# Layer 2's first tasks: half 1's sums to GpSimd, small products and weight sums later, values copied ahead of keys

## The chip, the core and the metric

The kernel runs on one core of a Trainium2 chip. The core has five engines, each with its own in-order instruction queue: TensorE (PE, matrix products; its weight loads are listed as PEld), VectorE (DVE), ScalarE (ACT), GpSimd (POOL) and SyncE (SP, which here only starts DMAs). They meet through semaphores. PE writes its results into PSUM, a small memory of eight banks; here each bank has a letter (S, U, T, V, X, Y, Z, W). DVE and ACT read PSUM; POOL does not. Everything else lies in SBUF or in device memory. The metric is the time of one execution in microseconds (us) of the device; lower is better.

## The reference, cut to what matters

Four transformer layers work on x, of 4 sequences of 256 tokens with 512 features, in fp32. In each, `x = x + attention(norm(x)) + ffn(norm(x))`. The change concerns layer 2 alone:

```python
# attention: 32 query heads, 8 key/value heads of 128 features, rotary, causal
qkv = einsum('bsh,oh->bso', xn, Wqkv)
xq, xk = rope(xq), rope(xk)
probs = softmax(where(causal, xq @ xk.T / sqrt(128), -1e30))
attn = (probs @ xv) @ Wo.T
# ffn: a dense product, and a mixture of 8 experts of rank 16
result = einsum('bsd,od->bso', xn, W_base) + b_base
ax = einsum('bsd,rd->bsr', xn, A_w)
probs = softmax(einsum('bsd,ed->bse', xn, router_w))
mixed = einsum('bseq,bse->bsq', einsum('bsr,erq->bseq', ax, cores), probs)
result = result + einsum('bsr,or->bso', mixed, B_w) * 2
```

## The kernel before, in words

The normalised input lies transposed in `xT`, features on partitions, 1024 tokens along the free axis. Its tokens are cut into half 0 (sequences 0 and 1) and half 1 (sequences 2 and 3); tiles 0 to 3 of 128 tokens are half 0, tiles 4 to 7 half 1.

All large products of layer 2 are done as 2 by 2 blocks with seven block products instead of eight (L1121, `SEVEN`). Each needs sums of blocks on both sides. For the input they are `s1` to `s4` (`summed`, L1134, four 128x512 additions, called for a half by `block_sums`, L1242); for a weight they are `t1` to `t4` (`Blocks.sums`, four additions on POOL). The seven products go to banks X, Y, Z, W, X, Z, W. `quarters` (L1369) says how four result quarters come out of them: ACT copies X into `u` and Z into `z`, DVE adds Y to `u`, then makes `c` = u + W (`c22`), POOL adds z to it: that is quarter (1,1). Later X is quarter (0,0), and Z and W, after DVE has added u, are (0,1) and (1,0). A function `place` empties each quarter: for queries the rotary (three DVE instructions and one addition on POOL); for keys and values (`key_tasks`, L1508) the rotary of the keys (`rotary_by_four`: three DVE instructions, L1463 once and L1461 twice, then an addition on POOL, L1487) and one ACT copy of the values (L1512). Keys and values of one quarter share a bank, and a tile `kv`, of which each takes a half.

The order of work on PE, DVE, ACT and POOL is written out by hand (`manual_schedule`, L1315): they execute in program order. SP is not in that list; a planner orders its DMAs. Program order comes from slots: `run` (L1929) takes a list of tasks, one a slot. In each slot it calls the task (a block product on PE), and then the functions that `after(k, f)` (L1350) has put down for that slot, k slots ahead, in the order in which they were put down. What the set-up puts down before the first slot therefore stands at the head of a slot's list. `spread(k, steps)` puts steps into successive slots.

Slots 0 to 6 are keys and values of key/value pair 0 for half 0 (`key_tasks(0, 0)`), slots 7 to 13 queries of half 0 (`query_tasks(0)`), slots 14 to 20 keys and values of half 1, 21 to 27 queries of half 1, 28 to 34 the base weight's output product of half 0. From slot 14 on attention runs beside this: `scores` of a head pair on PE in slot 14, 19, 24, 29, at once `masked` on DVE, a slot later `exponentials` on ACT, then `normalise`, then `turned_blocks` (DVE, and four DMAs on SP), then `values` on PE.

The first slots also carry what half 1 and the feed-forward part need: in slot 0 the moments of tiles 4 to 7 (DVE, and a square root on ACT); in slots 1 to 4 their normalisation (DVE), transposes (PE) and evacuation to `xT` (`turned`, L153; `evac`, L95, sends even tiles to DVE, odd ones to ACT); in slot 5 `route(1)` (the rank and router products for half 1: PE, and ACT's copy `flat`), in slot 6 `route_back(1)` and DVE's s1 and s2, in slot 7 s3 and s4, the router's softmax (`chosen`, L1960, with an exponential on ACT) and `core` (one product on PE, one ACT copy). Slots 8 to 11 hold eight DVE instructions `products` (L1970), slots 10 and 12 their transposes `turn_z` (L1979: four on PE, one ACT copy to `zT`), slots 6 to 9 POOL's sums of the base weight (`outs[0].sums()`). ACT's functions lie in sets; another set means a table load (ACT_TABLE_LOAD).

Of the kernel before, what the change touches and what calls it, by code (L numbers as in the profile page):

```python
# [21 lines left out]
F32 = mybir.dt.float32  # L22
# [4 lines left out]
AF = mybir.ActivationFunctionType  # L27
# [4 lines left out]
P = 128  # L32
B, T, C = 4, 256, 512
NT = B * T // P
# [22 lines left out]
def block_stack(ctx: ExitStack, tc: tile.TileContext, d: dict, out: bass.AP):  # L57
    nc = tc.nc

    const = ctx.enter_context(tc.tile_pool(name="const", bufs=1))  # L60
    small = ctx.enter_context(tc.tile_pool(name="small", bufs=4))
# [33 lines left out]
    def evac(i, dst, src):  # L95
        if i % 2:
            nc.scalar.copy(dst, src)
        else:
            nc.vector.tensor_copy(dst, src)
# [10 lines left out]
    xT = const.tile([P, NC, B * T], F32, name="xT")  # L110
# [18 lines left out]
    def moments(tiles):  # L129

        n = len(tiles)
        mv = small.tile([P, n, 2], F32, tag=f"mv{n}", name=f"mv_{tiles[0]}")
        for i, t in enumerate(tiles):
            st = small.tile([P, 6], F32, tag="st", name=f"st_{t}")
            nc.vector.bn_stats(st, x_sb[:, t, :])
            nc.vector.bn_aggr(mv[:, i, :], st)
        rstd = small.tile([P, n], F32, tag=f"rstd{n}", name=f"rstd_{tiles[0]}")
        nc.scalar.activation(rstd, mv[:, :, 1], AF.Sqrt, bias=eps, scale=1.0)
        nc.vector.reciprocal(rstd, rstd)
        return {t: (mv[:, i, 0:1], rstd[:, i : i + 1]) for i, t in enumerate(tiles)}  # L140

    def normed(t, moments, patterns):

        xn = lnp.tile([P, C], F32, tag="xn", name=f"xn_{t}")
        dst, src = xn, x_sb[:, t, :]
        if patterns:
            before, after, sizes = patterns
            dst = xn.rearrange(after, **sizes)
            src = src.rearrange(before, **sizes)
        nc.vector.tensor_scalar(dst, src, *moments[t], ALU.subtract, ALU.mult)  # L150
        return xn

    def turned(t, xn, tag="T"):  # L153

        tp = ps(tag, [P, NC, P], f"lnT_{t}")
        for c in range(NC):
            nc.tensor.transpose(tp[:, c, :], xn[:, c * P : (c + 1) * P], ident)
        evac(t, xT[:, :, t * P : (t + 1) * P], tp)


    def layer0_attention(hook, aside, xp, wd):
# [1025 lines left out]
    class Layer2Weights:  # L1187
# [51 lines left out]
                )  # L1239
            nc.scalar.copy(self.routed[:, 4 * half : 4 * half + 4, :], tp)  # L1240

        def block_sums(self, half):  # L1242
            A = self.A[half]
            for i in range(2):
                cols = slice((2 * half + i) * T, (2 * half + i + 1) * T)
                for j in range(2):
                    A[f"a{i + 1}{j + 1}"] = xT[:, 2 * j : 2 * j + 2, cols]
            return summed(
                nc.vector, A, lambda k: self.xs.tile([P, 2, T], F32, name=f"x_{k}_{half}")
            )  # L1250

        def first_half(self):
# [39 lines left out]
    def layers_2_and_3(w, late):  # L1292
# [8 lines left out]
        with ExitStack() as stack:  # L1301
# [25 lines left out]
            def tile2(tag, bufs, name):  # L1327
                pool = rp if tag in ("kv", "u", "z", "c", "t2") else lp
                return pool.tile([P, 2, T], F32, tag=tag, name=name, bufs=bufs)
# [8 lines left out]
            A = w.A  # L1338

            def turn_tile(t, mom):  # L1340
                turned(t, normed(t, mom, None), "TVSY"[t % 4])

            row = tile2("kv", 13, "b2_row").rearrange("p a i -> p (a i)")
            nc.sync.dma_start(out=row, in_=bc(d["b2"], 0, P))
# [5 lines left out]
            def after(k, *fs):  # L1350

                due.setdefault(slot[0] + k, []).extend(fs)
# [118 lines left out]
            def rotary_by_four(dst, src):  # L1471


                t2 = tile2("t2", 2, "t2")[:, 0, :]

                def natural(x):
                    return x.rearrange("p (x i b) -> p x b i", x=2, b=4)

                rotated(
                    dst.rearrange("p (x b i) -> p x b i", x=2, b=4),  # L1480
                    natural(src),
                    natural(rope[:, 0, :]),
                    natural(rope[:, 1, :]),
                    t2.rearrange("p (x b i) -> p x b i", x=2, b=4),
                    0,
                )
                after(1, lambda: nc.gpsimd.tensor_tensor(dst, dst, t2, ALU.add))  # L1487
# [20 lines left out]
            def key_tasks(gp, half):  # L1508
                def place(c, src):
                    t = kv[gp, half, c] = tile2("kv", 13, f"kv2_{gp}_{half}_{c[0]}{c[1]}")  # L1510
                    rotary_by_four(t[:, 0, :], src[:, 0, :])
                    nc.scalar.copy(t[:, 1, :], src[:, 1, :])  # L1512

                return quarters(lambda: A[half], lambda: w.sets["kv", gp].b, keys_values, place)

# [36 lines left out]
            class Layer3:  # L1552
# [241 lines left out]
                def turned(self, t, j, tag):  # L1794
                    half, i, tt = t // 4, t % 4 // 2, t % 2
                    A = self.retrieval[half]
                    tp = ps(tag, [P, 4, P], f"retT_{t}_{j}")
                    for k in range(4):
                        nc.tensor.transpose(tp[:, k, :], self.rets[t][4 * j + k], ident)  # L1799
                    key = f"a{i + 1}{j + 1}"  # L1800
                    if key not in A:
                        A[key] = self.rt[half].tile(
                            [P, 4, T], F32, tag="rt", name=f"rt_{half}_{key}", bufs=7
                        )
                    nc.vector.tensor_copy(A[key][:, :, tt * P : (tt + 1) * P], tp)
# [110 lines left out]
            def spread(k, steps):  # L1916

                for i, f in enumerate(steps):
                    after(k + i, f)
# [37 lines left out]
            zT = [tile2("kv", 13, f"zT_{i}").rearrange("p a i -> p (a i)") for i in range(2)]  # L1957
            core_out = tile2("kv", 13, "core_out_sb").rearrange("p a i -> p (a i)")

            def chosen():  # L1960
                nc.vector.tensor_reduce(most, probs, AX.X, ALU.max)
                nc.vector.tensor_tensor(probs, probs, bc(most, 2, EXPERTS), ALU.subtract)
                nc.scalar.activation(probs, probs, AF.Exp)
                nc.vector.tensor_reduce(most, probs, AX.X, ALU.add)
                nc.vector.reciprocal(most, most)
                nc.vector.tensor_tensor(probs, probs, bc(most, 2, EXPERTS), ALU.mult)
# [43 lines left out]
            def biased(t):  # L2010
                nc.gpsimd.tensor_tensor(x_sb[:, t, :], x_sb[:, t, :], row, ALU.add)

            half1 = {}
            after(0, lambda: half1.update(mom=moments(range(4, NT))))
            for i, t in enumerate(range(4, NT)):
                after(1 + i, lambda t=t: turn_tile(t, half1["mom"]))
            after(5, lambda: w.route(1, "U"), lambda: half1.update(sums=w.block_sums(1)))
            for i in range(4):
                after(6 + i // 2, lambda i=i: half1["sums"][i]())
            after(6, lambda: w.route_back(1, "S"))  # L2020
            after(7, chosen, core)
            for g in range(2):
                for i in range(4):
                    after(8 + 2 * g + i // 2, lambda t=4 * g + i: products(t))
                after(10 + 2 * g, lambda g=g: turn_z(g))
            spread(6, outs[0].sums())
            run(key_tasks(0, 0) + query_tasks(0))

            def next_set():
# [353 lines left out]
```

## Time and profile before

| What | us |
|---|---|
| Runs of the kernel | 1346.69, 1344.92, 1344.08 (median 1344.92) |
| Profiled execution | 1343.17 |
| its span on the core | 1341.4 |
| layer 2's first product (slot 0) starts | 488.21 |
| first queries (slot 7) start | 504.33 |
| first scores (slot 14) start | 523.71 |
| base weight's first product (slot 28) starts | 554.71 |

The table's slots are found in the timeline by the names of what a product writes and reads: `m<-xT,wkv_b` is a product of keys and values, `m<-xT,wq_b` one of queries, `s<-kv,q` scores, `m<-wo_b,xT` the output product. A timeline's line gives start, duration, engine, source line, operation, tiles, shapes, and in brackets the engine's idle time ahead of it with what ended it. Instructions of an engine overlap a little, so a duration is often some 0.1 us longer than the distance to the next start.

### The profile page before, as it was taken

How to read it: one execution, taken by the hardware profiler on the slowest of the kernel's cores; microseconds unless marked ns; L12 is line 12 of the kernel's file. 1: busy time of each engine (PE TensorE's matmuls, PEld its weight loads, DVE VectorE, ACT ScalarE, POOL GpSimd, SP SyncE). 2: the span in 40 equal slices, each digit the busy share in tenths (PEclk: the TensorE clock that was granted, in tenths of full speed). 3: DMA queues.
4: the chain of work that ended last, by engine and by line, in shares of the span. 5: the costliest groups of instructions: out<-in, count | busy, mean ns of one | idle time of the engine just before them, and what ended most of it. 6: DMA issues, size and time to landing. Idle time of an engine off the chain costs nothing. (4 is left out here: it accounts for less than half of the span.)

```text
span 1341.4 us, 20444 instructions
## 1 busy us (share of the span) xinstructions
PE 1300.8 (97%) x7076; PEld 1022.7 (76%) x7076; DVE 928.9 (69%) x1962; ACT 561.2 (42%) x1475; POOL 656.7 (49%) x662
## 2 busy tenths in 40 slices
PE   9999999899998998999999999999999999899998
PEld 7666665688445677888888888888888888677887
DVE  6676777488836449837877967777678776768654
ACT  2444445387012212433444443444534444655530
POOL 4555566478646014654575745747356563021410
PEclk9999999999999999999999999999999999999999
DMA  6012112300610021222433424433334333413001
GB/s 222 6 48 48 37 48 76 87 1 21 177 46 9 0 95 52 75 71 63 131 98 95 126 61 118 115 95 102 87 91 119 94 78 82 145 24 118 1 1 63
DMA packets 93480, 101.47 MB, mean 76 GB/s; under 512 B 21748, under 2 KB 66535, under 8 KB 92994
## 3 DMA queue, kind: packets, MB, share of 16 engines
q1 hardware_dynamic: 92450, 99.12, 26.1%
q8 instruction: 56, 0.92, 0.3%
q10 hardware_dynamic: 816, 0.79, 0.2%
q14 instruction: 46, 0.38, 0.1%
q0 software_dynamic: 112, 0.26, 0.1%
HBM read 67.06 MB, written 7.91 MB: 56 GB/s over the span
## 5 line engine op out<-in xcount | busy, mean ns | idle before, releaser
L1859 ACT ACTIVATE p<-p,nm 128x256 f32<-128x256 f32 (+1 forms) x256 | 113.3, 444 | 158.8 <-DVE nm L1843 158.0
L1456 POOL TENSOR_TENSOR q<-q,t 128x512 f32<-128x512 f32 x64 | 81.9, 1280 | 130.3 <-DVE t L1461 128.5
L1874 ACT ACTIVATE p<-p,rs 128x256 f32<-128x256 f32 (+1 forms) x256 | 95.5, 444 | 39.9 <-DVE rs L1870 39.9
L1406 PE MATMUL m<-xT,wq_b 128*128 128x256 f32 x448 | 103.9, 380 | 2.1 <-ACT kv L1512 2.0
L1461 DVE TENSOR_TENSOR t<-m,rope_sb 64x512 f32<-64x512 f32 (+1 forms) x144 | 95.3, 662 | 1.9
L1406 PEld LDWEIGHTS m<-xT,wq_b 128*128 128x128 f32 x448 | 82.6, 191 | 12.6 <-ACT kv L1512 2.4
L1389 POOL TENSOR_TENSOR c<-c,z 128x512 f32<-128x512 f32 x28 | 36.4, 1301 | 112.9 <-DVE c L1386 57.9
L1882 DVE STREAM_TRANSPOSE blocks<-p 128x768 f32<-128x768 f32 x64 | 62.6, 977 | 40.1 <-ACT p L1874 39.1
L1442 PE MATMUL m<-wo_b,o 128*128 128x256 f32 x384 | 89.6, 380 | 0.0
L1910 ACT COPY o<-av 128x512 f32<-128x512 f32 x64 | 37.2, 582 | 115.6 <-PE av L1900 110.1
L1843 DVE CUSTOM_DVE_ANT_0 p<-s,cmask 128x256 f32<-128x256 f32 (+1 forms) x256 | 76.1, 353 | 12.8 <-PE s L1824 11.1
L1521 DVE TENSOR_TENSOR x_sb<-x_sb,m 128x512 f32<-128x512 f32 x82 | 54.8, 679 | 36.6 <-PE m L1442 25.3
L1442 PEld LDWEIGHTS m<-wo_b,o 128*128 128x128 f32 x384 | 72.0, 191 | 9.1
L786 PE MATMUL dn<-wd,hT 128*128 128x512 f32 x176 | 76.4, 594 | 0.7 <-ACT o L782 0.7
L1406 PE MATMUL m<-x_s,wq_t 128*128 128x256 f32 x320 | 74.1, 381 | 2.4 <-ACT kv L1512 2.0
L843 POOL TENSOR_TENSOR sa<-sa,sb 128x1024 f32<-128x1024 f32 x22 | 62.1, 2824 | 29.0 <-DVE sb L838 29.0
L476 POOL TENSOR_SCALAR_AFFINE_SELECT keys<-keys 128x256 f32<-128x256 f32 x128 | 58.1, 467 | 28.9 <-ACT keys L472 28.8
L472 ACT ACTIVATE keys<-st 128x384 f32<-128x384 f32 x128 | 54.0, 488 | 40.1 <-PE st L462 40.1
L1406 PEld LDWEIGHTS m<-x_s,wq_t 128*128 128x128 f32 x320 | 60.3, 191 | 11.9 <-ACT kv L1512 2.4
L1899 PE MATMUL av<-q,kv 128*128 128x512 f32 x128 | 65.5, 594 | 1.6 <-DMA q<-blocks 1.6
L1824 PE MATMUL s<-kv,q 128*128 128x256 f32 x256 | 65.8, 380 | 0.4 <-POOL q L1456 0.4
L786 PEld LDWEIGHTS dn<-wd,hT 128*128 128x128 f32 x176 | 33.3, 190 | 41.1 <-issue 39.4
(329 smaller groups left out, 3272.9 us busy)
## 6 DMA issues: line engine op xcount, KB each, us to landing
q<-blocks SPq DMA_DIRECT2D x256, 96.0 KB
wq_b<-in_wq SPq DMA_DIRECT2D x38, 256.0 KB
wo_b<-in_wo SPq DMA_DIRECT2D x32, 256.0 KB
raw<-in_wo SPq DMA_DIRECT2D x24, 256.0 KB
wkv_b<-in_wkv SPq DMA_DIRECT2D x16, 256.0 KB
wos_d<-wos_row SPq DMA_DIRECT2D x28, 128.0 KB
gate_q<-in_gate_q SPq DMA_DIRECT2D x11, 256.0 KB
up_q<-in_up_q SPq DMA_DIRECT2D x11, 256.0 KB
```

The costliest lines, as they stand in the source:

```text
L786: nc.tensor.matmul(po, lhsT=hT[:, k, t * P : (t + 1) * P], rhs=wd[:, k, :], start=k == 0, stop=k == NBLK - 1,)
L843: nc.gpsimd.tensor_tensor(self.a, self.a, self.b, ALU.add)
L1406: nc.tensor.matmul(out[:, i, :], lhsT=b[:, c, i * P : (i + 1) * P], rhs=a[:, c, :], start=start and i == 0 and c == 0, stop=i == 1 and c == 1,
L1442: nc.tensor.matmul(out[:, t, :], lhsT=a[:, c, t * P : (t + 1) * P], rhs=b[:, c, :], start=start and t == 0 and c == 0, stop=t == 1 and c = ...
L1456: after(1 + 2 * pause, lambda: nc.gpsimd.tensor_tensor(dst, dst, t2, ALU.add))
L1461: nc.vector.tensor_tensor(t2[at], src[of], sin[of], ALU.mult)
L1824: nc.tensor.matmul(s1[:, i, :], lhsT=q[:, i, P:T], rhs=kt[:, 0, :], start=True, stop=True)
L1843: nc.vector.tensor_tensor_reduce(out=x[f"p{part}"][:, e, :], in0=x[f"s{part}"][:, e, :], in1=cmask if part else cmask[:, P : 2 * P], scale ...
L1859: nc.scalar.activation(p, p, AF.Exp, bias=x["nm"][:, part, e : e + 1], scale=-1.0, accum_out=x["sums"][:, part, e : e + 1],)
L1874: nc.scalar.activation(p, p, AF.Copy, scale=x["rs"][:, part, e : e + 1])
L1882: nc.vector.transpose(blocks, x["p"].rearrange("p e x (b i) -> p b (e x) i", b=4))
L1899: nc.tensor.matmul(av, lhsT=v[:, 0:P], rhs=q[:, :, :, 0:64], start=True, stop=False)
```

## The change

Seven edits, all in what the first slots of layer 2 hold:

- the evacuations of tiles 4 to 7 all go to ACT (`turned` takes the engine as `by`);
- a tiny exponential on ACT follows the moments in slot 0 (`begun`);
- `s1` to `s4` of half 1 go from DVE to POOL, and from slots 6 and 7 to slots 8 to 11;
- the router's softmax is cut in two: maximum, difference and exponential (`raised`) stay in slot 7, the sum and the division (`chosen`) go to slot 9;
- the eight `products` go to slots 11 to 18, one a slot, and the two `turn_z` to slots 16 and 20;
- the base weight's sums go to slots 15 to 18;
- for key/value pair 0, both halves, ACT's copy of the values comes ahead of DVE's rotary of the keys in program order.

```diff
-    def turned(t, xn, tag="T"):
+    def turned(t, xn, tag="T", by=None):
...
-        evac(t, xT[:, :, t * P : (t + 1) * P], tp)
+        evac(t if by is None else by, xT[:, :, t * P : (t + 1) * P], tp)
...
-        def block_sums(self, half):
+        def block_sums(self, half, eng=nc.vector):
...
-                nc.vector, A, lambda k: self.xs.tile([P, 2, T], F32, name=f"x_{k}_{half}")
+                eng, A, lambda k: self.xs.tile([P, 2, T], F32, name=f"x_{k}_{half}")
...
-                turned(t, normed(t, mom, None), "TVSY"[t % 4])
+                turned(t, normed(t, mom, None), "TVSY"[t % 4], 1)
...
                     t = kv[gp, half, c] = tile2("kv", 13, f"kv2_{gp}_{half}_{c[0]}{c[1]}")
+                    if gp == 0:
+                        nc.scalar.copy(t[:, 1, :], src[:, 1, :])
                     rotary_by_four(t[:, 0, :], src[:, 0, :])
-                    nc.scalar.copy(t[:, 1, :], src[:, 1, :])
+                    if gp:
+                        nc.scalar.copy(t[:, 1, :], src[:, 1, :])
...
-            def chosen():
+            def raised():
                 nc.vector.tensor_reduce(most, probs, AX.X, ALU.max)
                 nc.vector.tensor_tensor(probs, probs, bc(most, 2, EXPERTS), ALU.subtract)
                 nc.scalar.activation(probs, probs, AF.Exp)
+
+            def chosen():
                 nc.vector.tensor_reduce(most, probs, AX.X, ALU.add)
                 nc.vector.reciprocal(most, most)
                 nc.vector.tensor_tensor(probs, probs, bc(most, 2, EXPERTS), ALU.mult)
...
+            def begun():
+                half1.update(mom=moments(range(4, NT)))
+                nc.scalar.activation(small.tile([P, 1], F32, tag="table", name="table", bufs=1), eps, AF.Exp)
+
             half1 = {}
-            after(0, lambda: half1.update(mom=moments(range(4, NT))))
+            after(0, begun)
             for i, t in enumerate(range(4, NT)):
                 after(1 + i, lambda t=t: turn_tile(t, half1["mom"]))
-            after(5, lambda: w.route(1, "U"), lambda: half1.update(sums=w.block_sums(1)))
+            after(5, lambda: w.route(1, "U"), lambda: half1.update(sums=w.block_sums(1, nc.gpsimd)))
             for i in range(4):
-                after(6 + i // 2, lambda i=i: half1["sums"][i]())
+                after(8 + i, lambda i=i: half1["sums"][i]())
             after(6, lambda: w.route_back(1, "S"))
-            after(7, chosen, core)
+            after(7, raised, core)
+            after(9, chosen)
+            for t in range(NT):
+                after(11 + t, lambda t=t: products(t))
             for g in range(2):
-                for i in range(4):
-                    after(8 + 2 * g + i // 2, lambda t=4 * g + i: products(t))
-                after(10 + 2 * g, lambda g=g: turn_z(g))
-            spread(6, outs[0].sums())
+                after(16 + 4 * g, lambda g=g: turn_z(g))
+            spread(15, outs[0].sums())
             run(key_tasks(0, 0) + query_tasks(0))
```

## The prediction

> **What bounds the kernel now.** I read the page first, then the waits of TensorE (PE) from 484 us on, then each engine's timeline between 488 and 550 us, and last the groups that VectorE (DVE), ScalarE (ACT) and GpSimd (POOL) run there. The page: PE is busy nearly all the span, at full clock.
>
> ```profile
> span 1341.4 us, 20444 instructions
> PE 1300.8 (97%) x7076; PEld 1022.7 (76%) x7076; DVE 928.9 (69%) x1962; ACT 561.2 (42%) x1475; POOL 656.7 (49%) x662
> PEclk9999999999999999999999999999999999999999
> ```
>
> So a microsecond counts only where PE waits. PE's waits, 484 to 600 us (waiter, releaser: total, times, longest):
>
> ```profile
> PE m L1406 <- ACT kv L1512: 3.9, 2, 2.0
> PE m L1418 <- issue: 0.9, 1, 0.9
> PE s L1824 <- POOL q L1456: 0.4, 1, 0.4
> ```
>
> The 0.9 lies ahead of all that is changed. The rest, 4.37 us (2.00+1.95+0.42), could give at most 0.33%. From 524 us PE has no wait until 1146.88, so what is won or lost here reaches the end. PE's timeline (start, duration; wait before it):
>
> ```profile
> 504.33 1.97 PE L1406 MATMUL m<-xT,wq_b 128*128 128x256 f32 x8
> 506.24 1.12 PE L1990 MATMUL core_out<-bw_sb,cores_sb 16*128 16x512 f32 x2
> 507.29 2.00 PE L1406 MATMUL m<-x_s,wq_t 128*128 128x256 f32 x8
> 511.28 2.00 PE L1406 MATMUL m<-x_s,wq_t 128*128 128x256 f32 x8 [2.00 <-ACT kv L1512]
> 515.23 1.99 PE L1406 MATMUL m<-xT,wq_b 128*128 128x256 f32 x8 [1.95 <-ACT kv L1512]
> ```
>
> These are the first queries' products X, (core), Y, Z, W. Z and W wait until their bank is emptied of keys and values: three DVE instructions turn the keys, then ACT copies the values. ACT's timeline:
>
> ```profile
> 501.83 0.58 ACT L1227 COPY flat<-flat_b 128x512 f32<-128x512 f32 x1 [2.22 <-PE flat_b L1219]
> 502.31 0.38 ACT L1512 COPY kv<-m 128x256 f32<-128x256 f32 x1
> 506.80 1.28 ACT L1963 ACT_TABLE_LOAD   x1 [2.04 <-DVE routed L1962]
> 508.26 0.57 ACT L1993 COPY core_out_sb<-core_out 128x512 f32<-128x512 f32 x1
> 510.86 0.37 ACT L1512 COPY kv<-m 128x256 f32<-128x256 f32 x1 [2.03 <-DVE t L1461]
> ```
>
> The last row is the key: the copy writes its own half of a tile and reads its own half of the bank, yet starts 0.03 us after the last key instruction (509.63 to 510.83), though that writes another tile. The group of these copies says the same: of 32, 22 waited for DVE, 44.6 us. The copies whose source lies in SBUF do not: one starts at 518.19, inside the key instructions of 516.75 to 518.65. So DVE and ACT do not read one PSUM bank together; whoever is first in program order goes first.
>
> **The change, step by step.** Names: keys of quarter (0,0), (0,1), (1,0), (1,1) leave banks X, Z, W and tile c.
>
> *Off DVE, free on PE.* Two of four evacuations (0.69 each) go to ACT (0.59), the table load (1.28) to 489.4, behind the square root. ACT's first evacuation waits for PE until 492.4; it then delays the copy of u from 490.3 to 492.9, whose bank PE wants at 496.6; z's copy ends at 497.9, its bank is wanted at 498.8. Cost 0; if that cover were gone, at most the 2.6 us shift of u. No DMA moves with these.
>
> *Later work.* The base weight's sums are first read at 554.71 and zT at 565.94, so their lateness itself costs 0.
>
> *The sums of half 1* leave DVE (1.34+1.10+1.15+1.75 = 5.3 us, 500.5 to 506.3) for POOL, four times 1.27. Not needed before slot 15 (526 us), hence 0 as a due time; as company it costs, below.
>
> *Keys of (0,0), slot 5.* The copy stands behind `flat` and still runs at 502.31 to 502.68. New: DVE waits for it; the keys, at 498.58 before, start at 502.7, take 1.8 (509.02 to 510.83) and end at 504.5. X was wanted at 504.33: wait 0.2. Behind the keys in DVE's queue stand Z's addition and the softmax's first two, with slack.
>
> *Keys of (0,1), slot 7.* In ACT's queue the copy stands behind the copy of `core`, which needs PE's core product (now to 507.6). It starts 0.48 behind (501.83 to 502.31), ends at 508.5; keys to 510.35; PE is through with Y at 509.4: Z waits 1.0 instead of 2.00. DVE idles from the early softmax to 508.5; that is where the freed 5.3 us go.
>
> *Keys of (1,0).* Addition 0.68 to 511.05, copy 0.37, keys 1.8, to 513.3. PE, through with Z at 512.3, waits 1.05 instead of 1.95.
>
> *Keys of (1,1) to the first scores.* DVE: end of the softmax 0.75, u's addition 0.6, then keys from c, both inputs in SBUF. There POOL runs the sums. What that does stands in the rows of before: at 502.4 to 506.3 DVE's sums and POOL's took turns whole (DVE 1.75 for an instruction that takes 0.69 alone). Two of three key instructions waiting up to 1.1 gives 3.4 instead of 1.9: to 518.2. A product 0.2, c22 0.6: 519.1, where PE wants bank W at 518.7: wait 0.4. Product, three query rotations (2.0), POOL's addition 1.27: 522.6, where PE is ready at 521.0: wait 1.6 instead of 0.42.
>
> So the scores start at 522.6, 1.1 earlier, but the two transposes of z (0.44 each) have moved behind them: 0.2 won.
>
> *Slot 20.* DVE had 1 us of idle time between the two c22 at 519.63 and 533.76. Now it also takes seven products (0.2 each) and the collisions with POOL's base weight sums (four times 1.27, moved to slots 15 to 18): two of the query instructions reading c, near 1.1 each, and three products near 0.5. Together 4 us more on 13; half 1's c22 ends at 537.4, bank W is wanted at 536.55: wait 0.85.
>
> *Slot 23.* At slot 20 ACT's list begins with the copy of zT, waiting for PE's transposes after that slot's product; the exponentials of head pair 1 stand behind it, then the normalisation, then the values' copy of (0,1), and now DVE's keys wait for that copy. From the transposes' end: copy 0.5, exponentials 1.8 (536.80 to 538.6), sums' reciprocal 0.3, normalisation 1.5, copy 0.4, keys 1.8, latencies 0.2: 6.5 us. PE has queries X, attention values, queries Y: 1.73+1.29+1.73 = 4.75 before it wants bank Z. Wait 1.8. Before, keys and normalisation ran side by side:
>
> ```profile
> 538.91 1.49 ACT L1874 ACTIVATE p<-p,rs 128x256 f32<-128x256 f32 x4 [0.24 <-DVE rs L1870]
> 540.72 0.37 ACT L1512 COPY kv<-m 128x256 f32<-128x256 f32 x1 [0.32 <-DVE t L1461]
> ```
>
> *SP.* The two `pk` loads wait for the transposes of z (517.73 and 4 us later, before); they go out later, ahead of nothing due soon if the planner keeps them in order: 0. If not, see rival 3.
>
> **Sum.** Waits: 0.2+1.0+1.05+0.4+1.6+0.85+1.8 = 6.9, and each restart of PE costs 0.1 (eight matmuls took 2.00 after a wait, 1.89 without): 7.6. Before: 4.37+0.3 = 4.67. The kernel gets slower by 2.9 us. The profiled execution was 1343.17 us (span 1341.4 and 1.8 around it), so it becomes 1346.1; the median of the runs, 1344.92, stands 1.75 above, and becomes 1347.8.
>
> Bounds of what no row prices: collisions between none and one on every SBUF instruction move the waits 0.4, 1.6, 0.85 to 0, 0.1, 0 or 1.0, 2.4, 1.8; hand-overs move the others by 0.3 to 0.4 each. That gives 4.0 to 11 of waits, minus 0.7 to plus 6.3 us: 1344.2 to 1351.2. I take the middle, since the mixture in 500 to 520 us of before showed collisions in about half the places.
>
> **A rule weighed.** The rows show the order DVE, then ACT; the reverse order, on which the 0.2, the 1.8 and the late DVE hang, has no row here that had to wait. The Trainium skill, PSUM — Partial Sum Buffer, section "PSUM bank collisions raise a hardware error", says that the compiler back end puts a dependency between any two instructions of different engines on one bank, reads alike, ACT with DVE too. By the rule the sum is the one above; by the rows alone it could also be rival 1's. The rule speaks against this change.
>
> **Rivals.**
> 1. *Faster.* DVE does not wait for the earlier copy. Then the keys of (0,0) run at 498.6, those of (0,1) from 505.7, and Z and W are free in time; left are the first scores' wait (1.1, PE being ahead) and slot 20 (0.85): 2.2 with restarts against 4.67, 2.5 less; without collisions 4.6 less. About 1341.3. For it: a reader need not exclude a reader. Against: 22 of 32 copies waited exactly so. It decides if a key instruction starts before its quarter's copy ends.
> 2. *No change.* The order holds, but POOL and DVE meet less: the first scores wait 0.5, slot 20 not at all. Then 0.5 to 1.5 slower, near 1346. For it: POOL's sums start as soon as their queue lets them, some in DVE's idle time. Against: DVE is busy without a gap from 513 on.
> 3. *Much slower.* A `pk` load stands ahead of the first head's four loads of turned blocks in SP's queue and waits for the second transpose: these, at 532.26 before, go out at 540, land some 4.5 us later (1142.5 to 1146.9 for one set that was waited for), PE wants them at 541.5: 3 us more, 1350.8. Against: slots 16 and 20 alternate with slots 17 and 22 of the block loads.
> 4. *The table load is not moved* (put before the later exponential all the same): it would delay the copy of (0,1) by 0.5; 1348.3. The square root's load at 470.21, well ahead of its use, speaks for its moving.
>
> **How the numbers follow.** Differences under 0.2% (2.7 us) can't be told from none. Forecast 0.62, of which 0.45 lies beyond plus 2.7 us and 0.17 below; rival 2 0.17; rival 1 0.14, split 0.11 faster and 0.03 same; rivals 3 and 4 0.07, slower. So faster 0.11, same 0.37, slower 0.52. The forecast's own range is 1344.2 to 1351.2; to leave out no more than 2 in 10 the range goes from 1342.4 (into rival 1) to 1351.3.
>
> **What would show it.** Right: key instructions of L1463 starting just after L1512's copies (near 502.7, 508.5, 511.5); DVE idle near 506 to 508; the first scores near 522.6; a new wait of PE near 544 for DVE's keys, another near 536 for c22. Wrong, if DVE's keys overlap the copies, if PE shows no wait after the first scores, or if PE waits for a DMA near 541.

## The result and the profile after

The changed kernel takes 1347.28 us (median of 21 runs, 1345.49 to 1348.98); the kernel before, run beside it, takes 1345.12 us (21 runs, 1343.96 to 1346.95). The ratio is 1.0017, with a 95% interval of 1.0011 to 1.0023. So the change costs about 2.2 us: slower, as forecast, and by a little less than the 2.9 us of the sum. That is less than the 0.2% below which the prediction meant to call two kernels the same, but the interval leaves out 1.

The profiled run took 1346.22 us. The page of the kernel after (span, then busy time, share of the span and instructions of each engine):

```profile
span 1344.3 us, 20448 instructions
PE 1301.7 (97%) x7076; PEld 1022.8 (76%) x7076; DVE 926.8 (69%) x1956; ACT 562.0 (42%) x1478; POOL 660.3 (49%) x666
```

No engine has become the bound: DVE has 2 us less to do and POOL 4 us more. The difference is in when PE may run. The waits of PE after, 484 to 600 us (waiter, releaser: total, times, longest):

```profile
PE m L1406 <- DVE t L1461: 3.5, 3, 1.6
PE s L1827 <- POOL q L1456: 1.7, 1, 1.7
PE m L1418 <- DVE c L1386: 1.0, 1, 1.0
PE m L1418 <- issue: 0.9, 1, 0.9
PE m L1406 <- ACT routed L1240: 0.3, 1, 0.3
PE m L1406 <- DVE c L1386: 0.2, 1, 0.2
```

Before, PE waited for ACT's copies of values (3.9 us in two waits). After, the same banks are waited for with DVE's key instruction (L1461) as the last to leave them, and three further waits have appeared. PE's timeline after shows each at its place (start, duration; wait before it and what ended it):

```profile
504.83 1.97 PE L1406 MATMUL m<-xT,wq_b 128*128 128x256 f32 x8 [0.33 <-ACT routed L1240]
506.73 1.12 PE L1995 MATMUL core_out<-bw_sb,cores_sb 16*128 16x512 f32 x2
507.78 1.99 PE L1406 MATMUL m<-x_s,wq_t 128*128 128x256 f32 x8
510.76 1.97 PE L1406 MATMUL m<-x_s,wq_t 128*128 128x256 f32 x8 [0.99 <-DVE t L1461]
513.64 3.69 PE L1406 MATMUL m<-xT,wq_b 128*128 128x256 f32 x16 [0.92 <-DVE t L1461]
...
519.24 1.99 PE L1406 MATMUL m<-xT,wq_t 128*128 128x256 f32 x8 [0.17 <-DVE c L1386]
522.89 1.13 PE L1827 MATMUL s<-kv,q 128*128 128x256 f32 x4 [1.66 <-POOL q L1456]
...
537.77 1.13 PE L1418 MATMUL m<-xT,wkv_t 128*128 128x256 f32 x4 [1.02 <-DVE c L1386]
...
546.59 1.96 PE L1406 MATMUL m<-x_s,wq_t 128*128 128x256 f32 x8 [1.62 <-DVE t L1461]
```

In order: X, core, Y, Z, W, then slot 13, the first scores, slot 20 and slot 23. The waits add up to 6.71 us against 4.37 before.

The name beside X's wait misleads. In the version of the first experiment below, X starts at 504.01 and ACT's router copy (L1240) only at 504.20, so X does not need it. What X waits for after are the keys of (0,0), whose last instructions end at 503.36+1.21 = 504.57, and 0.26 us of hand-over.

Why the keys are late is in DVE's timeline after:

```profile
502.73 0.62 DVE L1463 TENSOR_TENSOR kv<-m,rope_sb 128x256 f32<-128x256 f32 x1 [5.64 <-ACT kv L1512]
503.36 1.21 DVE L1461 TENSOR_TENSOR t<-m,rope_sb 64x256 f32<-64x256 f32 x2
...
508.78 0.62 DVE L1463 TENSOR_TENSOR kv<-m,rope_sb 128x256 f32<-128x256 f32 x1 [2.09 <-ACT kv L1512]
...
511.66 0.62 DVE L1463 TENSOR_TENSOR kv<-m,rope_sb 128x256 f32<-128x256 f32 x1 [0.44 <-ACT kv L1512]
...
514.90 1.12 DVE L1463 TENSOR_TENSOR kv<-c,rope_sb 128x256 f32<-128x256 f32 x1
516.03 2.23 DVE L1461 TENSOR_TENSOR t<-c,rope_sb 64x256 f32<-64x256 f32 x2
```

and in ACT's, over the same stretch:

```profile
501.84 0.58 ACT L1227 COPY flat<-flat_b 128x512 f32<-128x512 f32 x1 [2.22 <-PE flat_b L1219]
502.32 0.38 ACT L1512 COPY kv<-m 128x256 f32<-128x256 f32 x1
...
507.88 0.59 ACT L1998 COPY core_out_sb<-core_out 128x512 f32<-128x512 f32 x1 [0.85 <-PE core_out L1995]
508.37 0.38 ACT L1512 COPY kv<-m 128x256 f32<-128x256 f32 x1
```

Read them together. DVE's keys start at 502.73, when the copy (502.32+0.38 = 502.70) is over, and at 508.78 behind 508.37+0.38 = 508.75. Each copy itself stands behind another copy of ACT that waits for PE: `flat` in the first case, `core` in the second. DVE idles 5.64 us and 2.09 us for a copy of 0.38 us (of the 5.64 it would have idled 1.50 for PE's product in any case, as the first experiment shows). The group of these copies (L1512) after, who waited for it, in us and times:

```profile
  DVE kv L1463: 10.0, 4
```

For comparisons between kernels I take the length of the stage, from the start of slot 0's first matmul to the start of slot 28's product with the output weight (L1442). It is 66.50 us before (488.21 to 554.71) and 70.04 after (488.23 to 558.27): 3.54 longer. A total time also holds what changes elsewhere from one execution to the next, as the last section shows. The span is only 2.9 longer: late in the program PE waits at two places for turned blocks to land, and the second came 5.77 us behind a product's start before (1155.75 to 1161.52) and 5.43 after (1159.32 to 1164.75), which gives back 0.34, and 0.3 more goes behind it.

### The profile page after: what moved, and what is told of

It is laid out like the page before. It is cut to its first block, busy times and chain, and to the rows that moved or that the text cites. A ratio compares the mean times of both kernels' runs of the same rounds, so it can differ in the third digit from the quotient of the medians.

```text
span 1344.3 us, 20448 instructions
## 1 busy us (share of the span) xinstructions
PE 1301.7 (97%) x7076; PEld 1022.8 (76%) x7076; DVE 926.8 (69%) x1956; ACT 562.0 (42%) x1478; POOL 660.3 (49%) x666
## 5 line engine op out<-in xcount | busy, mean ns | idle before, releaser
L1456 POOL TENSOR_TENSOR q<-q,t 128x512 f32<-128x512 f32 x64 | 81.5, 1273 | 129.2 <-DVE t L1461 127.7
L1461 DVE TENSOR_TENSOR t<-m,rope_sb 64x512 f32<-64x512 f32 (+1 forms) x144 | 95.3, 661 | 1.9
L1442 PE MATMUL m<-wo_b,o 128*128 128x256 f32 x384 | 89.6, 379 | 0.0
L1442 PEld LDWEIGHTS m<-wo_b,o 128*128 128x128 f32 x384 | 71.9, 190 | 9.1
```

The costliest lines, as they stand in the source:

```text
L1442: nc.tensor.matmul(out[:, t, :], lhsT=a[:, c, t * P : (t + 1) * P], rhs=b[:, c, :], start=start and t == 0 and c == 0, stop=t == 1 and c = ...
L1456: after(1 + 2 * pause, lambda: nc.gpsimd.tensor_tensor(dst, dst, t2, ALU.add))
L1461: nc.vector.tensor_tensor(t2[at], src[of], sin[of], ALU.mult)
```

## Experiments

The theory: the copies ahead of the keys are the loss. ACT and DVE do not read one PSUM bank together, program order decides who goes first, and ACT's queue at that place is later than DVE's. The other edits, taken together, should gain about 2 us, as the expectation of the first experiment has it. The rivals: the loss comes from POOL and DVE meeting in SBUF (moved sums), or from what was moved behind the first scores.

### Copy behind the keys again, all else as in the change

```
                 def place(c, src):
                     t = kv[gp, half, c] = tile2(...)
-                    if gp == 0:
-                        nc.scalar.copy(t[:, 1, :], src[:, 1, :])
                     rotary_by_four(t[:, 0, :], src[:, 0, :])
-                    if gp:
-                        nc.scalar.copy(t[:, 1, :], src[:, 1, :])
+                    nc.scalar.copy(t[:, 1, :], src[:, 1, :])
```

> The changed kernel, but with the values' copy behind the keys again, for both halves. Theory (the exclusive PSUM bank: DVE's keys wait for an earlier copy, and that copy stands behind other work in ACT's queue): queries Z and W no longer wait, the first scores start near 518.8 us with a wait of about 1.1 us, slot 20 waits about 0.9, slot 23 about 0.3; the base weight's first product starts near 552.6 us instead of 558.3 (changed) and 554.7 (before). Time: 2 us less than before, about 0.15%. Rival (the loss comes from POOL's sums meeting DVE, the copy's place matters little): first scores near 522 us, slot 28 near 558, about 2 us more than before.

The stage took 64.54 us: 5.50 less than after, and 1.96 less than before. The time was 1340.43 us against 1346.0, ratio 0.9965 (0.9953 to 0.9978). A second measurement of the same kernel:

> The changed kernel with the copy behind the keys for both halves, run again beside the last kernel. Theory: as in its first run the stage is 1.96 us shorter than before (64.54 instead of 66.50), 0.15%; the rest of its first measured gain (0.35%) was not made in this stage but by a late wait for a transfer near 1160 us, which was 0.66 in the profile of before and none in that run, and by the chip's run to run spread, so the ratio should come out between 0.996 and 0.9995. Rival (the stage hides more than its waits show): the ratio stays at 0.9965 or below.

It gave a stage of 64.58 and 1341.64 us, ratio 0.9975 (0.9965 to 0.9986), inside the range expected. So both agree that the remaining edits, taken together, make the kernel faster; which of them does, these two runs don't tell apart. DVE's timeline in the first of them:

```profile
498.26 0.63 DVE L1463 TENSOR_TENSOR kv<-m,rope_sb 128x256 f32<-128x256 f32 x1 [1.50 <-PE m L1428]
...
504.87 0.60 DVE L1463 TENSOR_TENSOR kv<-m,rope_sb 128x256 f32<-128x256 f32 x1
```

The keys of (0,0) wait for PE's matmul and no longer for ACT; counted from slot 0, which starts at 487.89 here, they run 4.1 us sooner than after. Those of (0,1) start at 504.87, ahead of the copy of `core`, 3.6 us sooner. PE's waits in this version, 484 to 600 us:

```profile
PE m L1418 <- DVE c L1386: 1.0, 1, 1.0
PE s L1824 <- POOL q L1456: 1.0, 1, 1.0
PE m L1418 <- issue: 0.9, 1, 0.9
```

X, Z, W and slot 23 wait for nothing. Beside the 0.9 ahead of slot 0, two waits are left, of slot 20 and of the first scores; the experiments on POOL's sums below bear on both. The copies follow the keys, at 507.55 for (0,1), and nothing waits long for them, because PE wants that bank only at 508.7. ACT once waits 1.33 us for DVE's keys, which costs PE nothing: what counts is which engine is late at the place.

### The copy ahead alone, in the kernel before

```
                     t = kv[gp, half, c] = tile2(...)
+                    if gp == 0:
+                        nc.scalar.copy(t[:, 1, :], src[:, 1, :])
                     rotary_by_four(t[:, 0, :], src[:, 0, :])
-                    nc.scalar.copy(t[:, 1, :], src[:, 1, :])
+                    if gp:
+                        nc.scalar.copy(t[:, 1, :], src[:, 1, :])
```

> The kernel before, with only the values' copy put ahead of the keys for key/value pair 0. Theory (exclusive bank): the keys of (0,0) start near 502.7 us instead of 498.6, those of (0,1) after the copy of core; queries Z wait about 5 us, W about 2; the first scores start near 526.5 and slot 28 near 558; 3 to 3.5 us more than before, about 0.25%. Rival (POOL's sums meeting DVE are the loss): nothing of that is moved here, so within 0.5 us of before.

Stage 70.04 us, 3.54 more than before; 1348.85 us, ratio 1.0023 (1.0014 to 1.0031). By itself this edit costs as much as the whole change. ACT's timeline here shows what the copy of (0,1) stands behind:

```profile
512.95 1.28 ACT L1966 ACT_TABLE_LOAD   x1 [5.47 <-DVE routed L1965]
...
514.40 0.57 ACT L1996 COPY core_out_sb<-core_out 128x512 f32<-128x512 f32 x1
514.87 0.38 ACT L1512 COPY kv<-m 128x256 f32<-128x256 f32 x1
```

DVE's sums of half 1, still on DVE in this kernel, now run behind the late keys of (0,0), from 507.30 to 512.48; the softmax of the experts stands behind them; ACT's exponential and its table load wait for that softmax; and the copy stands behind all of it. The keys of (0,1) start at 515.27 and PE's Z waits 4.76 us. But DVE's own part of that softmax stands ahead of these keys too, and it ends when the copy does (515.02+0.23 = 515.25, and 514.87+0.38 = 515.25):

```profile
505.42 0.62 DVE L1463 TENSOR_TENSOR kv<-m,rope_sb 128x256 f32<-128x256 f32 x1 [4.15 <-ACT kv L1512]
...
515.02 0.23 DVE L1969 TENSOR_TENSOR routed<-routed,most 128x64 f32<-128x64 f32 x1
```

So what Z waits for here is handed on from the first copy ahead, which made DVE idle 4.15 us; the second copy adds nothing to it. In the full change, with the sums on POOL and the table loaded early, Z waits 0.99 instead, but the first scores, slot 20 and slot 23 wait longer, and the stage comes out the same. Why the waits that PE lists here are too few for the stage stands under "What was not expected of the hardware".

The same trace answers another question. The copy and the first key instruction write the same tile `kv`, each its own half, so the tile might be what orders them, and not the bank. For quarter (1,1) both read tile c, which lies in SBUF:

```profile
523.02 0.62 DVE L1463 TENSOR_TENSOR kv<-c,rope_sb 128x256 f32<-128x256 f32 x1
524.54 0.40 ACT L1512 COPY kv<-c 128x256 f32<-128x256 f32 x1
```

The copy is first in program order here too, yet the keys start 1.52 us ahead of it. Without a common PSUM bank there is no waiting.

### The copy ahead for half 0 only

```
-                    if gp == 0:
+                    if (gp, half) == (0, 0):
                         nc.scalar.copy(t[:, 1, :], src[:, 1, :])
                     rotary_by_four(t[:, 0, :], src[:, 0, :])
-                    if gp:
+                    if (gp, half) != (0, 0):
```

> The changed kernel, with the copy ahead of the keys for half 0 alone; half 1's keys come first again. Theory: everything up to slot 20 as in the changed kernel (first scores 522.9 us, wait 1.0 in slot 20); in slot 23 the wait falls from 1.6 to about 0.3 us, slot 28 starts near 556.8; 1.4 us less than the changed kernel. Rival (the late copy of zT ahead of the exponentials makes the wait of slot 23, whatever the order of keys and values): the wait stays near 1.6.

Stage 68.50, 1.54 less than after. The wait of slot 23 is gone altogether, and all others stay (0.33, 0.97, 0.93, 0.19, 1.66, 1.04). So of the 5.50, half 1's copies cost 1.54, and 3.96 are left for half 0's. The time, 1346.57 us, ratio 1.0006 (0.9997 to 1.0014), can't be told from before's.

For slot 23, ACT's timeline after is the chain that the prediction named:

```profile
540.26 0.60 ACT L1989 ACTIVATE zT<-zT 128x512 f32<-128x512 f32 x1 [6.17 <-PE zT L1988]
540.76 0.50 ACT L1862 ACTIVATE p<-p,nm 128x256 f32<-128x256 f32 x1
...
542.85 1.49 ACT L1877 ACTIVATE p<-p,rs 128x256 f32<-128x256 f32 x4 [0.25 <-DVE rs L1873]
544.25 0.35 ACT L1512 COPY kv<-m 128x256 f32<-128x256 f32 x1
```

zT's copy, exponentials, normalisation, values' copy: 4.34 us from the first start to the last end, and DVE's keys only then, at 544.63.

### The second transpose of z three slots later

```
-                after(16 + 4 * g, lambda g=g: turn_z(g))
+                after(16 + 7 * g, lambda g=g: turn_z(g))
```

> The changed kernel with the second transpose of z in slot 23 instead of 20. Theory: in slot 20 ACT's copy of zT, waiting for PE, no longer stands ahead of the exponentials, so they start when their maxima are there, near 540.0 us instead of 540.76; the wait of slot 23 falls from 1.62 to between 0.9 and 1.2, not to zero, because the keys still stand behind the values' copy and that behind the normalisation. Rival (the copy of zT is the whole cause of slot 23): no wait there.

The wait of slot 23 went from 1.62 to 1.29, and not to 0: taking zT's copy out lets the exponentials start 0.66 us sooner (51.87 us behind slot 0 instead of 52.53), not more, since they also wait for DVE's maxima. That is above the 0.9 to 1.2 expected, because PE too reaches this place 0.30 us sooner, without the transposes ahead of it (Y of slot 22 starts 54.55 us behind slot 0 instead of 54.85). The stage is 0.57 shorter (69.47).

### Half 1's sums two slots sooner

```
             for i in range(4):
-                after(8 + i, lambda i=i: half1["sums"][i]())
+                after(6 + i, lambda i=i: half1["sums"][i]())
```

> The changed kernel with half 1's sums on POOL in slots 6 to 9 instead of 8 to 11. Theory (the last two sums collide with the keys that are read from c): these three key instructions take about 1.9 us instead of the 3.4 of the changed kernel, the wait of 0.17 in slot 13 goes, the first scores' wait falls from 1.66 to about 0.6, and slot 28 starts some 1.2 to 1.6 us sooner after slot 0 than 70.04. Rival (the first scores are late for the products in DVE's queue): the wait stays above 1.4.

Stage 68.57: 1.47 less. The keys that are read from tile c lie at the same place in DVE's timeline here,

```profile
514.84 0.60 DVE L1463 TENSOR_TENSOR kv<-c,rope_sb 128x256 f32<-128x256 f32 x1
515.46 1.24 DVE L1461 TENSOR_TENSOR t<-c,rope_sb 64x256 f32<-64x256 f32 x2
```

and take 1.84 us instead of the 3.35 of after (1.12+2.23). POOL's last two sums, which lay beside them in POOL's timeline after,

```profile
514.26 1.27 POOL L1144 TENSOR_TENSOR xT<-xT 128x512 f32<-128x512 f32 x1
515.49 1.67 POOL L1140 TENSOR_TENSOR x_s<-xT,x_s 128x512 f32<-128x512 f32 x1
```

are through at 512.6 here. Slot 13's wait is gone and that of the first scores falls from 1.66 to 0.60. So the collision was about as large as the prediction put it, and it was avoidable: POOL was idle for 5.39 us ahead of 504.65 after, room for the first of the four sums.

### The base weight's sums five slots later

```
-            spread(15, outs[0].sums())
+            spread(20, outs[0].sums())
```

> The changed kernel with the base weight's sums in slots 20 to 23 instead of 15 to 18. Theory (POOL's sums meet DVE's instructions with both inputs in SBUF and make DVE late for bank W in slot 20): DVE's two long instructions there (1.76 us for the first of the query from c, 1.53 for the second) fall to about 0.7, the wait of slot 20 goes from 1.02 to 0, slot 28 starts 1.0 us sooner after slot 0 than the 70.04 us of the changed kernel. Rival (the eight products alone make DVE late): the wait falls by less than 0.3.

Stage 68.80, 1.24 less; slot 20's wait went from 1.02 to 0. The cost was right, one detail was not. Two of DVE's query instructions that read tile c took 1.76 and 1.53 us after; here the second takes 0.69, while the first stays at 1.76. It starts 0.16 us behind a POOL instruction of 1.37 us that is part of the queries themselves (L1456, 529.79 in the trace after), so moving the weight's sums can't free it. Nor did the second lie beside one of these sums after: it started at 534.37, beside POOL's addition L2016 (534.09, 1.26 us), which the sums had held up in POOL's queue. Without them that addition runs at 531.53, in a trace whose slot 0 starts 1.07 us later.

### The exponential table where it was

```
             def begun():
                 half1.update(mom=moments(range(4, NT)))
-                nc.scalar.activation(small.tile([P, 1], F32, tag="table", ...), eps, AF.Exp)
```

> The changed kernel without the tiny exponential of slot 0, so that the table is loaded ahead of the router's exponential in slot 7. Theory: the load of 1.28 us ends near 508.1 us, the copies of core and of the values slip by some 0.45, so do the keys, and queries Z wait 1.4 to 1.5 instead of 0.99; slot 28 starts 0.3 to 0.5 us later after slot 0 than 70.04. Rival (the load is hidden in either place, since ACT waits there for PE's core product anyway): no difference above 0.1.

Stage 70.39, 0.35 more. The load is back at 506.92, ahead of the copies of `core` (508.38) and of the values (508.84); Z's wait grows from 0.99 to 1.28, less than the 1.4 to 1.5 expected. So loading the table sooner is worth about 0.3 us here, where the values' copy stands behind it; without the copy ahead it was not tried.

### The small work later still, and all of it together

Without the copies ahead, two more versions move what is not needed until slot 28:

```
             for t in range(NT):
-                after(11 + t, lambda t=t: products(t))
+                after(21 + t, lambda t=t: products(t))
             for g in range(2):
-                after(16 + 4 * g, lambda g=g: turn_z(g))
-            spread(15, outs[0].sums())
+                after(25 + 5 * g, lambda g=g: turn_z(g))
+            spread(21, outs[0].sums())
```

> As the run with the copy behind the keys, and the eight products go to slots 21 to 28, their transposes to slots 25 and 30, the base weight's sums to slots 21 to 24. Theory: DVE is the late one in slots 11 to 20, and the products and the collisions with the base weight's sums are what it has too much; without them the first scores start near 518.4 us, slots 20 and 23 wait for nothing, slot 28 starts near 550.3, 4.4 us earlier than before; 4 us less than before, about 0.3%. Rival (the small work only moves its cost to slots 21 to 30, where DVE is as full): slot 28 near 552.5, as with the copy alone.

Stage 61.90, 4.60 less than before. The first scores wait 0.62; slot 20 waits no more. The time was 1341.12 us, ratio 0.9962 (0.9949 to 0.9974). A part of the gain is only put off: one transpose of z and a wait of 0.33 us now lie behind slot 28, and at the later heads 3.45 us are left of the 4.60. The second version adds half 1's sums two slots sooner and moves the rest a little further:

```
             for i in range(4):
-                after(8 + i, lambda i=i: half1["sums"][i]())
+                after(6 + i, lambda i=i: half1["sums"][i]())
...
+                after(23 + t, lambda t=t: products(t))
...
+                after(27 + 4 * g, lambda g=g: turn_z(g))
+            spread(21, outs[0].sums())
```

> Copy behind the keys as before, half 1's sums on POOL in slots 6 to 9, products in slots 23 to 30, their transposes in slots 27 and 31, base weight's sums in slots 21 to 24. Theory: almost no wait is left up to slot 28 (0.2 at the first scores), so slot 28 starts about 61.4 us after slot 0 (66.50 before, 70.04 changed, 64.54 with the copy behind the keys alone), and heads after it keep 3.8 to 4.2 us on before, the transposes of z having moved behind slot 26. Time: 4 us less than before, about 0.3%. Rival (work moved into slots 21 to 31 costs there what it saves): the later heads keep no more than the 1.95 us of the copy behind the keys alone.

Stage 61.22, 5.28 less than before, and from slot 0 to slot 28 PE waits for nothing. Of PE's waits from 484 to 600 us only the one ahead of slot 0 is left:

```profile
PE m L1418 <- issue: 0.9, 1, 0.9
```

The later heads keep 4.78 us, more than the 3.8 to 4.2 expected. The time is 1339.62 us (five runs, 1337.52 to 1341.09) against 1345.39: ratio 0.9956 (0.9944 to 0.9969). This version beats both kernels. It keeps the sums on POOL and the early table, and drops the copy ahead. Of its 5.28 us, 1.96 come from the change without the copy ahead, 2.64 from the small work moved later, and 0.68 from the sums' two slots and the last moves together.

### All stages side by side

| kernel | stage, us | against before | against after | ratio to before, 95% |
|---|---|---|---|---|
| before | 66.50 | | -3.54 | |
| after | 70.04 | +3.54 | | 1.0011 to 1.0023 |
| copy behind the keys again | 64.54, 64.58 | -1.96, -1.92 | -5.50, -5.46 | 0.9953 to 0.9978, 0.9965 to 0.9986 |
| copy ahead alone | 70.04 | +3.54 | 0 | 1.0014 to 1.0031 |
| ahead for half 0 only | 68.50 | +2.00 | -1.54 | 0.9997 to 1.0014 |
| weight's sums five slots later | 68.80 | +2.30 | -1.24 | one run |
| second transpose later | 69.47 | +2.97 | -0.57 | one run |
| half 1's sums sooner | 68.57 | +2.07 | -1.47 | one run |
| table where it was | 70.39 | +3.89 | +0.35 | one run |
| copy behind, small work later | 61.90 | -4.60 | -8.14 | 0.9949 to 0.9974 |
| the same, sums sooner | 61.22 | -5.28 | -8.82 | 0.9944 to 0.9969 |

The stages come from one execution each. Twice measured, "copy behind" gives 64.54 and 64.58, and a wait that an edit leaves alone comes out the same within 0.04 us from trace to trace (W's 0.92 to 0.94, the first scores' 1.65 and 1.66).

For the versions with more than one run, stage and ratio agree in order but not in size: by the medians, 1346.57-1346.0 = 0.6 us for "half 0 only" where the stage gives 2.0, and 1346.0-1340.43 = 5.6 us less for "copy behind" where it gives 1.96 (3.8 less in its second measurement). Why the totals stray by up to 3.6 us is not settled; two things that vary between executions are shown below.

## Why the prediction was right

**The mechanism held.** Sign, place and cause of the loss are as forecast, and the Trainium skill's rule on bank collisions (PSUM — Partial Sum Buffer, "PSUM bank collisions raise a hardware error") agrees with what the runs show: it tells of a dependency between two engines on one bank, readers too, and here the second reader waits in this order as well. After, no key instruction that reads a bank starts before its quarter's copy ends (502.73 behind 502.70, 508.78 behind 508.75), so rival 1 is out. The 1341.3 it named is close to what the version without the copies ahead reached (1340.43 and 1341.64), because there DVE indeed does not wait.

**The waits, one by one** (forecast, then measured): X 0.2, 0.33; Z 1.0, 0.99; W 1.05, 0.92; slot 13 0.4, 0.17; first scores 1.6, 1.66 (at 522.89 for 522.6); slot 20 0.85, 1.02; slot 23 1.8, 1.62. Sum 6.9, 6.71. The collisions that had no row of their own came out at the middle that was taken: 3.35 us for the keys from c where 3.4 was put, 1.76 and 1.53 for the two query instructions, though neither lay beside one of the weight's sums. Slot 20's 0.85 does not follow as written: "4 us more on 13" from 519.1 gives 536.1, ahead of the 536.55 at which PE wants the bank. The 537.4 needs the 4 on top of the whole 14.13 us between the two c22 of before; that distance was 18.53 after (518.50 to 537.03), 4.40 more. The lower bound of 4.0 is too high as well: with 0.3 off each of the four other waits and collisions at their least, the terms give 4.05-1.2+0.1 = 2.95 of waits, and at most 0.7 for restarts. The result does not turn on that bound.

**The term that was mis-sized** is "each restart of PE costs 0.1 (eight matmuls took 2.00 after a wait, 1.89 without)". Both durations were read off the rows, but 1.89 holds a modelled end that overlaps the next product. Products that stream start 1.72 us apart, as the starts before show and the durations don't:

```profile
517.50 1.89 PE L1406 MATMUL m<-xT,wq_b 128*128 128x256 f32 x8
519.22 1.89 PE L1406 MATMUL m<-x_s,wq_b 128*128 128x256 f32 x8
```

After, the product at 519.24 restarts PE and is followed at 522.89 with a wait of 1.66 between, so 3.65-1.72-1.66 = 0.27 is lost besides the wait. Seven waits after and three before make (6.71+7x0.27)-(4.37+3x0.27) = 3.4 us, against 3.54 of the stage. With 0.1 the sum gives 2.7. Had 0.27 been taken, the forecast would have been 3.6 for the stage.

**That the time came out at 2.2 and not 3.5** is no merit of the sum. Of the 3.54 us in the stage the profiled execution gave back 0.64 behind 1155 us, and the medians differ by 2.16. The profiled execution's 1346.22, where 1346.1 was forecast, is luck: restarts priced too low and that 0.64 nearly cancel. The forecast that "what is won or lost here reaches the end" was therefore right only to within about 1 us: there is a later place where PE waits for a transfer, and it was on the list of waits of before.

**The rivals.** Rival 2 (fewer collisions, no change): the collisions were there, 1.47 and 1.24 us by the experiments that remove them one at a time. Rival 3 (a `pk` load ahead of the block loads): the two loads went out at 530.26 and 540.32 and the blocks at 534.36 between them, and PE had no wait near 541. Rival 4 (the table load not moved): it was moved, to 489.42; leaving it costs 0.35, where 0.5 was put.

**What the sum did not see** is how its parts stand to each other. It put the change down as one loss of 2.9 spread over seven waits. In fact the copy ahead costs 5.50 within the change and hides a gain of 1.96 from the other edits. Of the 5.3 us of sums taken off DVE it said only that they go into DVE's idle time; rival 1, which priced the change without that waiting at 2.5 us less, had the gain. How much of the 1.96 the sums make, and how much the other edits, was not measured.

## What to carry to other kernels

Where two engines read one PSUM bank, the order in the program decides who waits, so put first the engine whose queue is free at that moment; look at what stands ahead of the short instruction in its own queue, not at its length. Sums moved to POOL cost time here where they ran beside DVE's work with both inputs in SBUF, and two slots decided that. Price a restart of PE from the starts of neighbouring products, not from their durations.

## What was not expected of the hardware

**Half the clock after a wait.** In the kernel with the copy ahead alone, Z's product takes 3.75 us:

```profile
517.23 3.75 PE L1406 MATMUL m<-x_s,wq_t 128*128 128x256 f32 x8 [4.76 <-DVE t L1461]
521.19 2.38 PE L1406 MATMUL m<-xT,wq_b 128*128 128x256 f32 x8 [0.21 <-DVE t L1461]
```

The windows of the same trace (us; busy time and instructions of PE, PEld, DVE, ACT, POOL; granted clock; DMA share; GB/s) give the reason:

```profile
514.00:516.00 2.00, 0.00 (x0) 0.00 (x0) 1.36 (x5) 1.23 (x4) 0.00 (x0) 0.80 0.00 0
516.00:518.00 2.00, 0.77 (x2) 0.71 (x3) 1.96 (x5) 0.28 (x2) 0.84 (x2) 0.50 0.00 0
521.75:522.33 0.58, 0.58 (x3) 0.53 (x2) 0.58 (x2) 0.00 (x0) 0.20 (x1) 0.75 0.00 0
```

Taking the 0.80 and the 0.75 as mixtures of 1.00 and 0.50, the clock is halved from 515.2 to 522.04, 6.8 us. W could not have started sooner anyway, since DVE's keys for it end at 521.05; so the slow Z hides a wait of about 1.8 us, and only some 0.4 us of the product at 521.19 is lost to the clock. That is why this kernel's listed waits, 5.63 us, are too few for its stage.

The same happens behind a wait of 2.6 us that every version has late in the program. A product there takes 5.41 us after and 3.72 with the small work later:

```profile
1159.32 5.41 PE L1442 MATMUL m<-wo_t,o_s 128*128 128x256 f32 x16 [2.58 <-DVE o_s L1140]
```

```profile
1154.67 3.72 PE L1442 MATMUL m<-wo_t,o_s 128*128 128x256 f32 x16 [2.60 <-DVE o_s L1140]
```

From its windows the clock after was halved from 1160.7 to 1164.1, 3.4 us, beginning 1.3 us behind PE's restart. Seven of the twelve traces show such a stretch, five show none. In the kernel before it begins 0.6 us ahead of the restart. The waits are 2.52 to 2.63 us in all of them, so the wait's length does not decide it. The Trainium skill (TensorE: Matmul & The Clock Gate, "Part 1: The HAM clock gate (the "warmup" mystery)") tells of a free-running activity window of 3.4 us, and of a halved clock after an idle one; both lengths seen fit one and two such windows. It asks for an idle window of that length, though, and here a wait of 2.58 us was enough in some executions.

**A landing that varies.** Behind that product PE waits for blocks: the time from the product's start to the attention product behind it was 5.22 to 6.62 us over the twelve traces, at full clock (5.22, 5.74, 6.62) as at half (5.25, 5.77, 6.25). The wait written there, 0 to 2.90 us, is thus mostly a matter of how long the product took. What moves the landing itself by up to 1.4 us was not tried.

**The start of the stage**, ahead of which no edit changes anything, came in three groups over the twelve traces, and the granted clock from 60 to 120 us (in three windows of 20 us) falls into the same three:

| granted clock, 60 to 80, to 100, to 120 us | slot 0 starts at, us | traces |
|---|---|---|
| 1.00, 1.00, 1.00 | 487.89 to 488.48 | before, after, copy behind (both), sums sooner, table where it was |
| 1.00, 0.92 or 0.93, 0.99 | 488.88, 489.30 | half 0 only, weight's sums later |
| 0.91, 0.96 or 0.97, 0.94 or 0.95 | 490.56 to 490.92 | copy ahead alone, second transpose later, both with small work later |

So 2 to 3 us of a total time go with where the clock is halved in a stretch that none of the edits touches. The time of the profiled execution less its stage follows the same groups: 1275.6 to 1276.7, then 1277.0 and 1277.2, then 1278.5 to 1280.3 us. That the clock changes from execution to execution of one kernel is on record too: of 23 runs of the kernel before, the fastest, 1342.06 us, had a mean granted clock of 0.998, and the slowest, 1347.37, one of 0.993. That is a good part of what makes totals stray from the stages, and the reason for comparing stages; that it is all of it is not shown.
